# Pacing the modulation weight rows of a fused S4 + FFN kernel by product columns

## The chip, the cores and the metric

The kernel runs on one core of one Trainium2 chip. The time is device time in microseconds of one execution, the median of several; one more execution was recorded by the hardware profiler. Matrix products run on TensorE (PE), elementwise work on VectorE (DVE) and ScalarE (ACT), a few reductions over partitions on GpSimd (POOL). SyncE (SP) issues nearly all DMAs, in order: a DMA that waits for its data or its buffer holds back all that stand behind it.

## The reference, cut to what matters

x has 4 batches of 1024 channels by 2048 positions; c is 4 x 2048.

```python
mod = (_silu(c) @ wmod).reshape(4, 6, 1, -1)          # wmod: 2048 x (6*2048), 96 MB
sa, ca, ga, sb, cb, gb = (mod[:, i] for i in range(6))
# ga, gb: sign kept, magnitude at least 0.25
h = layernorm(x) * (1 + ca) + sa
x = x + ga * (causal_conv(h, K) + D[0] * h)           # K: S4 kernel of 2048 taps
h = layernorm(x) * (1 + cb) + sb
x = x + gb * (h @ W.T + bias + low_rank(h, A, Bf, coeffs * scales))
```

## The kernel before, in words

**Modulation rows.** The product with wmod is made in six sections (one for each of the six vectors) of 16 rows. A row is one load of 1 MB (`mod_load`, L309 to L313, tile `wm`, issued on SP) and four groups of products into the one PSUM tile `modps` (`mod_mm`, L317; eight matmul instructions in the profile). After the 16th row a section has a 17th step that turns `modps` into what is needed: columns `ca` (section 1), `sa` (section 0) or gates such as `gas` (section 2, `mod_gate`). The generator `section(sec, pools)` (L845) does one row for each `next`, and `take(g, n)` asks for n steps. Row buffers lie in two pools, `wmp` (three buffers) and `wms` (two); sections 1 and 0 alternate between them, sections 2 to 5 use `wmp` alone. A buffer is free when the products of its row are done.

**Convolution.** Channels are taken in 32 blocks of 128 rows. The causal convolution is a product with Toeplitz tiles of the taps, done with three products of halves in place of four, each operand split into two fp16 parts. For a block: `stats` (DVE), then `conv_prep` (normalize into `n`, transposes `tp`, scaling into `t`, the fp16 parts `hc` and `hs`), then `conv_mm` (L591): for each of two halves q, three families of matmuls (L608), into PSUM tiles `ya` and `yb`, drained by ACT (`qs`, L621, and L632 in early blocks) and DVE (L625 to L635). Five PSUM banks (`acc`) serve these, the merges (`lps`) and others. `conv_mm` calls `tick()` at nine places, where the caller slips other work into the program.

Blocks 0 to 2 are early: their gate is not there yet, so their products are kept in `y` (three buffers) and gated later by `conv_late` (L639). Blocks 0 and 1 are even run without `sa`; its share is added by `shift_conv` and `shift_add`. `conv_post` stores the gated block to `x1d` and squares into the x tile, after which block r+4 can be loaded into it.

**Kernel taps.** `toeplitz` (L233) computes the taps in steps woven into section 1 at rows `KT`. Its end is a chain through memory: `kd` is written (L253, L254), read back as overlapping rows `kb` (L258), both issued on ACT, multiplied with a reversal matrix (`kbps`) and split into `kh`, `kl`, which the first block's products need.

**Low-rank merge.** `prep_lora` (L418) loads `la` and `lb` (2 MB each) and works on them mostly on ACT. `merge` (L462), for eight column groups, makes the low-rank product (`lps`), adds it to W rows (`we`) and stores the combined weights of seven sub-products (`wcd`). The generator `rest` (L930) weaves merges and the rows of sections 4, 3 and 5; `step` (L974) advances it from block `R0` on, nine times a block by the strings of `PLAN`.

**Order.** The text order of the program is a priority. A scheduler in the framework places each instruction on its engine's list when by its own estimate its inputs are ready, the earlier in the text first. `high_priority` lifts a stretch over the rest, and `issue_after(ins)` keeps instructions on the engine of `ins` behind it. On the chip each engine then follows its list in order.

The feed-forward product (L744, blocks of `fX`, `fY`, `fZ`) follows after block 31.

Of the kernel before, what the change touches and what calls it, by code (L numbers as in the profile page):

```python
# [24 lines left out]
P = 128  # L25
# [9 lines left out]
class Net:  # L35
# [197 lines left out]
    def toeplitz(self, pool):  # L233
        nc, v = self.nc, self.nc.vector
        rev = pool.tile([P, P], F32, tag="rev", name="rev")
        nc.gpsimd.memset(rev, 0.0)
        nc.gpsimd.affine_select(
            out=rev, in_=rev, compare_op=ALU.not_equal, fill=1.0, base=1 - P, pattern=[[1, P]], channel_multiplier=1
        )
        kk = pool.tile([P, 16], F32, tag="kk", name="kk")  # L240
        yield from self.s4(pool)
        v.tensor_copy(kk, self.kp)
        dt = pool.tile([1, 1], F32, tag="dt", name="dt")
        nc.scalar.dma_start(out=dt, in_=self.io["D"].unsqueeze(0))
        v.tensor_tensor(kk[0:1, 0:1], kk[0:1, 0:1], dt, ADD)
        m = pool.tile([P, 1], F32, tag="km", name="km")
        v.tensor_reduce(m, kk, AX.X, ALU.max, apply_absolute_value=True)
        s, self.kinv = self.pow2(self.cst, self.allmax(pool, m, 1, "km"), 1, "ks")
        v.tensor_scalar(kk, kk, s, None, MUL)
        kd = self.dram.tile([P + D], F32, tag="kd", name="kd")  # L250
        z = pool.tile([1, P], F32, tag="kz", name="kz")
        v.memset(z, 0.0)
        nc.scalar.dma_start(out=kd[0:P].unsqueeze(0), in_=z)  # L253
        nc.scalar.dma_start(out=kd[P:].rearrange("(a b) -> a b", b=16), in_=kk)  # L254

        kb = pool.tile([P, D], F32, tag="kb", name="kb")
        src = bass.AP(tensor=kd.tensor, offset=kd.offset + 1, ap=[[1, P], [1, D]])
        nc.scalar.dma_start(out=kb, in_=src)  # L258
        self.kb = kb
        yield  # L260
        for q in range(4):
            ps = self.acc.tile([P, 512], F32, tag="a", name="kbps")
            nc.tensor.matmul(ps, rev, kb[:, ds(512 * q, 512)], start=True, stop=True)
            (v.tensor_copy if q % 2 else nc.scalar.copy)(kb[:, ds(512 * q, 512)], ps)


        kv = kb.rearrange("p (m e t) -> p m e t", e=2, t=P)
        ev, od = kv[:, :, 0, :], kv[:, :, 1, :]
        self.kf = {}
        for f in (0, 2, 1):  # L270
            hi = self.kpool.tile([P, HC * P], F16, tag=f"kh{f}", name=f"kh{f}")
            lo = self.kpool.tile([P, HC * P], F16, tag=f"kl{f}", name=f"kl{f}")
            h3, l3 = (x.rearrange("p (m t) -> p m t", t=P) for x in (hi, lo))
            if f == 0:
                src = ev
            else:
                src = pool.tile([P, 2, 512], F32, tag="kdif", name="kdif")
                src = src.rearrange("p a (c t) -> p (a c) t", t=P)
                if f == 1:
                    v.tensor_scalar(src[:, 0:1], ev[:, 0:1], -1.0, None, MUL)  # L280
                    v.tensor_tensor(src[:, 1:], od[:, 0 : HC - 1], ev[:, 1:], SUB)
                else:
                    v.tensor_tensor(src, od, ev, SUB)
            v.tensor_copy(h3, src)
            v.tensor_tensor(l3, src, h3, SUB)  # L285
            self.kf[f] = hi, lo
        yield
# [21 lines left out]
    def mod_load(self, pool, sec, j):  # L309
        w = pool.tile([P, D], F32, tag="wm", name="wm")  # L310
        src = self.io["wmod"].rearrange("(p j) n -> p j n", j=16)
        self.nc.sync.dma_start(out=w, in_=src[:, j, ds(sec * D, D)])
        return w  # L313

    def mod_mm(self, w, j):
# [272 lines left out]
                v.tensor_tensor(lo[:, sl], src, hi[:, sl], SUB)  # L588
            yield

    def conv_mm(self, pl, hs, x, tick, early):  # L591
        nc, v = self.nc, self.nc.vector
        hc, hs = hs
        y = pl["y"].tile([P, D], F32, tag="y", name="y")
        yv = y.rearrange("p (j e t) -> p j e t", e=2, t=P)
        if not early:
            gv = self.gat.rearrange("p (j e t) -> p j e t", e=2, t=P)
        sums = pl["sm"].tile([P, 2], F32, tag="sums", name="sums")

        def family(ps, f, q, first):  # L600
            pf = ps.rearrange("p j t -> p (j t)")
            last = 4 * q + 3
            for i in range(last + 1):
                o = P * max(0, i - 4 * q)
                k0 = P * max(0, 4 * q - i)
                for x, z in ((0, 0), (0, 1), (1, 0)):
                    h = hs[x][:, i] if f == 0 else hc[x][:, 2 * i + 2 - f]
                    nc.tensor.matmul(  # L608
                        pf[:, o:512], h, self.kf[f][z][:, ds(k0, 512 - o)],
                        start=first, stop=(i == last and (x, z) == (1, 0)), skip_group_check=True,  # L610
                    )
                    first = False
                if i == 3 and q == 1:
                    tick()

        for q in range(2):
            jj = slice(4 * q, 4 * q + 4)
            pa = self.acc.tile([P, 4, P], F32, tag="a", name="ya")
            family(pa, 0, q, True)
            qs = pl["t"].tile([P, 4, P], F32, tag="qs", name="qs")  # L620
            nc.scalar.copy(qs, pa)  # L621
            tick()
            pb = self.acc.tile([P, 4, P], F32, tag="a", name="yb")
            family(pb, 2, q, True)
            v.tensor_tensor(yv[:, jj, 1, :], pb, qs, ADD)  # L625
            if not early:
                v.tensor_tensor(yv[:, jj, 1, :], yv[:, jj, 1, :], gv[:, jj, 1, :], MUL)
            tick()
            family(pa, 1, q, False)
            sl = ds(1024 * q, 1024)  # L630
            if early:
                nc.scalar.copy(yv[:, jj, 0, :], pa)  # L632
            else:
                v.tensor_tensor(yv[:, jj, 0, :], pa, gv[:, jj, 0, :], MUL)  # L634
                v.scalar_tensor_tensor(y[:, sl], y[:, sl], 1.0, x[:, sl], MUL, ADD, accum_out=sums[:, q : q + 1])  # L635
            tick()
        return y, sums
# [167 lines left out]
ACC, TPS = 5, 2  # L805
PLAN = ("PNSL", "NL", "NSL", "NTL", "SL", "SL", "SL", "SL", "FSL", "SSL")
LPLAN = ("LL", "LL", "LL", "LL", "L", "0", "")
R0 = 3
WM, WMS = 3, 2
EARLY = 3  # L810
X0 = 11
LEFT0 = 30
KT = (0, 5, 7, 11)


def STQ(nc):
# [8 lines left out]
def net(ctx: ExitStack, tc: tile.TileContext, io):  # L825
# [19 lines left out]
    def section(sec, pools):  # L845
        for q in range(16):
            if q == 0:
                k.mod_begin()
            k.mod_mm(k.mod_load(pools[q % len(pools)], sec, q), q)
            yield  # L850
        if sec == 0:
            k.sa = k.mod_column(msm, k.kpool, "sa", 0.0)
            k.hinv = k.fold_scale(msm, k.ca, k.sa, "fs1")
        elif sec == 1:
            k.ca = k.mod_column(msm, k.kpool, "ca", 1.0)
        elif sec == 2:
            k.gas, (k.gad,) = k.mod_gate(msm, "gad")
        elif sec == 4:
            k.cb = k.mod_column(msm, k.cst, "cb", 1.0)
        elif sec == 3:  # L860
            k.sb = k.mod_column(msm, k.cst, "sb", 0.0)
        else:
            _, k.gbd = k.mod_gate(msm, "gbd", io["bias"])
        yield

    def merges():
        k.prep_lora(pl["lora"], pl["mrg"])
        yield
        for c in range(HC):
            yield from k.merge(pl["lora"], pl["mrg"], c)  # L870
# [3 lines left out]
    def take(g, n):  # L874
        for _ in range(n):
            next(g, None)
# [12 lines left out]
    def prep(r, shift=True):  # L889
        return k.conv_prep(pl, r, xs[r], sts.pop(r), hs, shift)  # L890

    def load(r):
        xs[r] = k.conv_load(pl, r)

    def stats(r):
        sts[r] = k.stats(pl, xs[r], "1")
# [8 lines left out]
        n += 1  # L905
    k.early_scale(msm)
    load(1)
    sec = section(0, (wms, wmp))
    for r in range(2):
        stats(r)  # L910
        take(prep(r, False), 9)
    take(sec, 1)
    with tc.issue_after(k.last.ins), tc.high_priority():
        take(toe, 2)
    take(sec, 1)

    def row():
        take(sec, 1)

    for r in range(2):  # L920
        ys[r] = k.conv_mm(pl, hs.pop(r), xs[r], row, True)
        load(r + 2)
    take(sec, 17)
    k.shift_conv(msm)
    k.shift_add([ys[r][0] for r in range(2)])
    st.close()
# [48 lines left out]
        if r >= R0 and "w" not in pr and next(fill, 0) == 0:  # L975
            early()

    sec = section(2, (wmp,))
    for r in range(2, EARLY + 1):
        stats(r)  # L980
    take(prep(2), 9)
    ys[2] = k.conv_mm(pl, hs.pop(2), xs[2], row, True)
    nxt = prep(3)
    take(nxt, 9)
    take(sec, 17)
    k.gat = k.gate_tile(pl["g"], 0)
    ratio = k.kpool.tile([P, 1], F32, tag="rat", name="rat")
    nc.vector.tensor_tensor(ratio, k.einv, k.hs[:, 0:1], MUL)
# [5 lines left out]
    stats(EARLY + 1)  # L994
    nxt = prep(EARLY + 1)
    take(nxt, 1)
    post = None
    for r in range(EARLY, 32):
        if EARLY + 2 < r + 2 < 32:
# [129 lines left out]
```

## Time and profile before

| | us |
|---|---|
| median of 3 runs (2148.76 to 2154.0) | 2149.32 |
| the profiled execution | 2149.26 |
| its span | 2147.5 |
| TensorE busy in the span | 2085.0 |
| VectorE busy | 1313.8 |
| ScalarE busy | 922.0 |
| data moved by DMA | 483.05 MB |

| stage before, from the trace | us from the span's start |
|---|---|
| last row of section 1 ends | 51.7 |
| block 0's first product | 66.6 |
| block 1's products end | 121.4 |
| block 2 | 136.7 to 161.0 |
| block 3 | 168.6 to 208.6 |
| last row of section 2 ends | 183.6 |
| block 4's first product | 227.5 |
| block 31's products end | 927.9 |

How to read the profile: it is one execution. A row of a group has the source line, the engine, the operation, output and inputs by name, shapes and count, then busy time and the mean of one in ns, then the idle time of the engine before these and what ended it. A row of waits reads "who <- for whom: us in total, times, longest". PEclk is the share of full clock that was granted to TensorE. Windows are in us from the span's start.

### The profile page before, as it was taken

What the parts mean: (1) busy time and instruction counts of PE and PEld (TensorE: products, weight loads), DVE (VectorE), ACT (ScalarE), POOL (GpSimd) and SP (SyncE); (2) the same over time, 40 slices, a digit from 0 to 9 for tenths busy, and PEclk for the clock granted to TensorE, in tenths of its full rate; (3) what the DMA queues carried; (4) which work ended last, traced back from release to release, by engine and by line L of the source; (5) the groups of instructions that cost most, each with busy time, mean ns of one, the idle gap of its engine ahead of it and who ended that gap; (6) DMA issues with size and microseconds to landing.
All of it is one profiled execution on the core that took longest, in us unless ns stands there. A gap on an engine that the chain in (4) does not pass through costs nothing.

```text
span 2147.5 us, 28491 instructions
## 1 busy us (share of the span) xinstructions
PE 2085.0 (97%) x11144; PEld 1028.0 (48%) x11144; DVE 1313.8 (61%) x2356; ACT 922.0 (43%) x1697; POOL 3.0 (0%) x13
## 2 busy tenths in 40 slices
PE   6998999999999999999999999999999999999999
PEld 2453445455455555554545545545444444444444
DVE  5636989988999998666566565565433323232323
ACT  1335757766677776655554454454200000000000
POOL 0000000000000000000000000000000000000000
PEclk7998999999999999999999999999999999999999
DMA  9878677767874463297465465564795545455542
GB/s 389 347 266 312 253 271 286 291 247 272 312 286 160 181 221 118 94 376 281 175 242 199 174 245 189 191 240 180 266 358 165 186 152 170 165 167 166 176 156 70
DMA packets 127142, 483.05 MB, mean 225 GB/s; under 512 B 13673, under 2 KB 13802, under 8 KB 96032
## 3 DMA queue, kind: packets, MB, share of 16 engines
q1 hardware_dynamic: 126192, 477.55, 61.1%
q10 hardware_dynamic: 816, 3.69, 0.4%
q8 instruction: 87, 1.43, 0.3%
q14 instruction: 47, 0.39, 0.0%
HBM read 325.89 MB, written 155.30 MB: 224 GB/s over the span
## 4 chain that ended last, share of the span: by engine, by line
PE 59%; DVE 6%; DMA 2%; ACT 2%; issue 1%; SPq 0%; DVEq 0%; ACTq 0%
PE fZ L744 23%; PE fY L744 15%; PE fX L744 15%; PE ya L608 3%; PE tp L694 2%; PE yb L608 1%; DVE y L635 1%; DMA xo<-x1d 1%; ACT x L654 1%; DVE wch L509 1%; DVE hc L588 1%; DVE st L535 1%; DMA w<-wcd 1%; ACT t L577 1%; DVE y L634 0%
## 5 line engine op out<-in xcount | busy, mean ns | idle before, releaser
L744 PEld LDWEIGHTS <-lf 128*128 128x128 f16 x5376 | 526.0, 98 | 620.5 <-issue 0.9
L744 PE MATMUL fZ<-w,lf 128*128 128x512 f16 x2304 | 514.1, 379 | 0.6 <-ACT p L752 0.6
L744 PE MATMUL fX<-w,lf 128*128 128x512 f16 x1536 | 342.1, 379 | 0.0
L744 PE MATMUL fY<-w,lf 128*128 128x512 f16 x1536 | 342.1, 379 | 0.0
L608 PEld LDWEIGHTS <-hc 128*128 128x128 f16 x2304 | 214.1, 98 | 208.7 <-issue 45.6
L762 DVE TENSOR_TENSOR xo<-xo,gb 128x512 f32<-128x512 f32 x128 | 87.7, 690 | 235.1 <-DMA xo<-x1d 223.6
L577 ACT ACTIVATE t<-tp,sa,ca 128x128 f32<-128x128 f32 x480 | 189.3, 474 | 20.2 <-PE tp L573 19.9
L608 PE MATMUL ya<-kh,hs 128*128 128x512 f16 (+3 forms) x768 | 195.0, 328 | 1.8 <-DVE hs L588 0.7
L608 PE MATMUL ya<-kh,hc 128*128 128x512 f16 (+3 forms) x768 | 191.7, 327 | 3.8 <-ACT qs L621 3.8
L608 PE MATMUL yb<-kh,hc 128*128 128x512 f16 (+3 forms) x768 | 190.8, 326 | 0.2
L752 ACT COPY p<-fZ 128x512 f32<-128x512 f32 x64 | 37.3, 583 | 292.6 <-PE fZ L744 275.3
L608 PEld LDWEIGHTS <-hs 128*128 128x128 f16 x1152 | 107.2, 98 | 104.2 <-issue 24.1
L696 ACT ACTIVATE gt<-tp,sb,cb 128x256 f32<-128x256 f32 x256 | 125.0, 576 | 62.5 <-PE tp L694 60.9
L752 ACT COPY p<-fX 128x512 f32<-128x512 f32 x32 | 18.8, 586 | 305.8 <-PE fX L744 227.3
L317 PE MATMUL modps<-wm,sct 128*32 128x512 f32 x768 | 119.7, 663 | 24.3 <-DMA wm<-in_wmod 16.0
L608 PE MATMUL ya<-kl,hs 128*128 128x512 f16 (+3 forms) x384 | 125.8, 328 | 0.7 <-DVE kl L285 0.7
L608 PE MATMUL ya<-kl,hc 128*128 128x512 f16 (+3 forms) x384 | 125.5, 327 | 0.0
L608 PE MATMUL yb<-kl,hc 128*128 128x512 f16 (+3 forms) x384 | 125.1, 326 | 0.0
L767 DVE TENSOR_TENSOR fin<-fX,gb 128x512 f32<-128x512 f32 x32 | 22.1, 692 | 127.3 <-PE fX L744 127.2
L481 PE MATMUL lps<-lbh,lac 128*128 128x512 f16 x256 | 87.4, 389 | 8.8 <-DVE y L634 3.3
L588 DVE TENSOR_TENSOR hc<-t,hc 128x512 f16<-128x512 f32 x128 | 87.7, 685 | 8.7 <-ACT hc L587 8.6
L573 PE MATMUL tp<-ident,n 128*128 128x128 f32 x512 | 79.2, 280 | 13.8 <-ACT t L577 9.8
(259 smaller groups left out, 2230.8 us busy)
## 6 DMA issues: line engine op xcount, KB each, us to landing
wm<-in_wmod SPq DMA_DIRECT2D x96, 1024.0 KB
lfd<-lf SPq DMA_DIRECT2D x112, 512.0 KB
lf<-lfd SPq DMA_DIRECT2D x112, 512.0 KB
x<-in_x SPq DMA_DIRECT2D x32, 1024.0 KB
x1d<-y SPq DMA_DIRECT2D x32, 1024.0 KB
x<-x1d SPq DMA_DIRECT2D x32, 1024.0 KB
xo<-x1d SPq DMA_DIRECT2D x128, 256.0 KB
out<-xo SPq DMA_DIRECT2D x128, 256.0 KB
```

The source lines that it names most:

```text
L317: self.last = self.nc.tensor.matmul(self.modps[32 * g : 32 * g + 32, :], self.sct[:, j].rearrange("p r b -> p (r b)"), w[:, ds(512 * g, 512)],
L481: nc.tensor.matmul(ps, la[:, x, k, h], y[:, k, osl], start=(n == 0), stop=(n == 5))
L573: nc.tensor.transpose(tp[:, k], n[:, ds(P * (c0 + k), P)], self.ident)
L577: nc.scalar.activation(t[:, k], tp[:, k], AF.Identity, bias=self.sa[:, c, b : b + 1], scale=self.ca[:, c, b : b + 1],)
L588: v.tensor_tensor(lo[:, sl], src, hi[:, sl], SUB)
L608: nc.tensor.matmul(pf[:, o:512], h, self.kf[f][z][:, ds(k0, 512 - o)], start=first, stop=(i == last and (x, z) == (1, 0)), skip_group_chec ...
L694: nc.tensor.transpose(tp[:, c, r], xs[r][:, ds(P * (c0 + c), P)], self.ident)
L696: nc.scalar.activation(t[:, c0 + c], tp[:, c], AF.Identity, bias=self.sb[:, c0 + c, b : b + 1], scale=self.cb[:, c0 + c, b : b + 1],)
L744: nc.tensor.matmul(ps[name], lf[i][:, k, x, :], wc[i][k // 4][:, k % 4, y, :], start=(first and n == 0), stop=(n == 3 * HC - 1), skip_grou ...
L752: nc.scalar.copy(t, ps[name])
L762: v.tensor_tensor(x, x, self.gbias[:, h], ADD)
L767: v.tensor_tensor(t, cv, self.gbt[:, h], MUL)
```

## The change

- The three DMAs of `kd` and `kb` are issued on POOL instead of ACT, and the third and fourth step of the tap computation stand one row earlier (`KT`).
- Sections 0 and 2 become one stream `rows`. It is no longer advanced at the ticks of the early blocks, but by `pace`, called after each set of matmuls of `conv_mm` with the number of columns multiplied: every `ROWC` = 3700 columns give one step. It runs through blocks 0, 1 and 2.
- Loads of blocks 0 to 3 are kept on SP behind the latest row load that the text has reached (`lastw`), and blocks 2 and 3 are asked for ahead of the products of blocks 0 and 1 instead of behind them.
- Statistics and preparation of block 2 stand ahead of the shift sums; those of block 3 go into the ticks of block 2.
- `prep_lora` is asked for once, by `next(fill)` ahead of the loop over blocks 3 to 31, and its SP loads stand behind the last row of section 2.
- The merges, and with them the rows of sections 4, 3 and 5, begin at block 5 instead of block 3 (`R0`).

```diff
@@ toeplitz
-        nc.scalar.dma_start(out=kd[0:P].unsqueeze(0), in_=z)
-        nc.scalar.dma_start(out=kd[P:].rearrange("(a b) -> a b", b=16), in_=kk)
+        nc.gpsimd.dma_start(out=kd[0:P].unsqueeze(0), in_=z)
+        nc.gpsimd.dma_start(out=kd[P:].rearrange("(a b) -> a b", b=16), in_=kk)
...
-        nc.scalar.dma_start(out=kb, in_=src)
+        nc.gpsimd.dma_start(out=kb, in_=src)
@@ mod_load
-        self.nc.sync.dma_start(out=w, in_=src[:, j, ds(sec * D, D)])
+        self.lastw = self.nc.sync.dma_start(out=w, in_=src[:, j, ds(sec * D, D)])
@@ conv_mm
-    def conv_mm(self, pl, hs, x, tick, early):
+    def conv_mm(self, pl, hs, x, tick, early, pace=lambda n: None):
...
                 if i == 3 and q == 1:
                     tick()
+                pace(3 * (512 - o))
@@ constants
-R0 = 3
+R0 = 5
+ROWC = 3700
-KT = (0, 5, 7, 11)
+KT = (0, 5, 6, 10)
@@ net: merges, load
-        k.prep_lora(pl["lora"], pl["mrg"])
+        with tc.issue_after(k.lastw.ins):
+            k.prep_lora(pl["lora"], pl["mrg"])
...
-        xs[r] = k.conv_load(pl, r)
+        if r < 4:
+            with tc.issue_after(k.lastw.ins):
+                xs[r] = k.conv_load(pl, r)
+        else:
+            xs[r] = k.conv_load(pl, r)
@@ net: blocks 0 and 1
-    sec = section(0, (wms, wmp))
+    rows = (x for sec, w in ((0, (wms, wmp)), (2, (wmp,))) for x in section(sec, w))
...
-    take(sec, 1)
+    take(rows, 1)
     with tc.issue_after(k.last.ins), tc.high_priority():
         take(toe, 2)
-    take(sec, 1)
-
-    def row():
-        take(sec, 1)
+    take(rows, 1)
+    cols = [0]
+
+    def pace(n):
+
+        cols[0] += n
+        while cols[0] >= ROWC:
+            cols[0] -= ROWC
+            take(rows, 1)
 
     for r in range(2):
-        ys[r] = k.conv_mm(pl, hs.pop(r), xs[r], row, True)
         load(r + 2)
-    take(sec, 17)
+        ys[r] = k.conv_mm(pl, hs.pop(r), xs[r], lambda: None, True, pace)
+    stats(2)
+    take(prep(2), 9)
     k.shift_conv(msm)
     k.shift_add([ys[r][0] for r in range(2)])
@@ net: block 2, ahead of the loop
-    sec = section(2, (wmp,))
-    for r in range(2, EARLY + 1):
-        stats(r)
-    take(prep(2), 9)
-    ys[2] = k.conv_mm(pl, hs.pop(2), xs[2], row, True)
+    stats(3)
     nxt = prep(3)
+    ys[2] = k.conv_mm(pl, hs.pop(2), xs[2], lambda: take(nxt, 1), True, pace)
     take(nxt, 9)
-    take(sec, 17)
+    take(rows, 40)
...
     take(nxt, 1)
+    next(fill)
     post = None
```

## The prediction

> **What bounds the kernel now.** I read the page's busy shares and slices first, then finer stretches of the first 400 us, then whom TensorE waited for in the stretch that stood out, then single rows of the timeline.
>
> ```profile
> PE 2085.0 (97%) x11144; PEld 1028.0 (48%) x11144; DVE 1313.8 (61%) x2356; ACT 922.0 (43%) x1697; POOL 3.0 (0%) x13
> PE   6998999999999999999999999999999999999999
> PEclk7998999999999999999999999999999999999999
> ```
>
> TensorE is busy 2085.0 of 2147.5 us. The change removes no product, so all that it can win is idle time (62.5 us in all) and time at a lowered clock. Both lie in the first slices. The next answer gives stretches of those: width, TensorE busy, granted clock, DMA share, GB/s.
>
> ```profile
> 16.00:56.00 40.00, 29.47 (x152) 0.67 0.99 403
> 66.00:136.00 70.00, 69.28 (x446) 0.98 0.78 295
> 136.00:158.00 22.00, 21.60 (x136) 1.00 0.72 279
> 158.00:186.00 28.00, 20.15 (x138) 0.89 0.99 368
> 186.00:197.00 11.00, 11.00 (x42) 0.83 0.70 270
> 197.00:213.00 16.00, 13.50 (x79) 1.00 0.70 251
> 213.00:224.00 11.00, 7.62 (x21) 0.53 0.99 371
> 224.00:262.00 38.00, 37.16 (x223) 1.00 0.59 227
> 278.00:284.00 6.00, 5.63 (x16) 0.72 0.65 257
> 284.00:400.00 116.00, 116.00 (x722) 1.00 0.73 269
> ```
>
> The reader is to see three regimes. To 56 us the DMA is full (0.99) and weight rows set the pace. From 66 to 158 TensorE is full while the DMA is only 0.72 to 0.78 busy: transfer time is thrown away. From 158 to 186 that is paid back: DMA full, TensorE waiting. Who it waits for from 136 to 290:
>
> ```profile
> PE modps L317 <- DMA wm<-in_wmod: 8.3, 7, 4.6
> PE lps L481 <- DVE y L634: 3.3, 1, 3.3
> PE lps L481 <- DVE y L625: 2.5, 1, 2.5
> PE tp L573 <- ACT t L577: 2.3, 2, 2.0
> PE lps L481 <- ACT lbh L456: 2.1, 1, 2.1
> PE lps L481 <- DVE we L483: 0.5, 1, 0.5
> ```
>
> With 0.3 us on hs these are 19.3 us of idle. Half clock adds: 1.4 in 158:186 (the last three rows took 1.56, 1.94 and 1.94 instead of 1.06), 11 x 0.17 = 1.9 in 186:197, 7.62 x 0.47 = 3.6 in 213:224, 6 x 0.28 = 1.7 in 278:284: 8.6 us. So 136 to 290 loses 27.9 us. 284:400 is full; the small waits later (some 16 us up to 960) I hold for unchanged by a shift of two blocks.
>
> **The change part by part.**
>
> *Paced rows.* A row of section 0 or 2 is one 1 MB load and 8 matmuls, 1.06 us together in the timeline. At 403 GB/s a load takes 1.049 MB / 403 = 2.60 us. A block's products have 3 x 3 x (1280 + 3328) = 41,472 columns (the two halves of L603 to L612), and 24 matmuls of 512 take 5.18 us in the chain, so a block is 17.5 us and 3,700 columns are 1.56 us. One row per 3,700 columns is thus a row per 1.56 + 1.06 = 2.62 us, just what the DMA delivers. Three blocks give 33.6 pulls; 32 are needed after the two taken ahead. The last row's matmuls fall at 92% of block 2. Before, 5 of the 16 gate rows were still to come when block 3 began (168.6 us). Now none is. Removed: the row waits from 158 to 183 (0.24 + 0.33 + 0.42 + 0.15 + 1.64 + 0.94 = 3.7) and the half clock they led to (1.4 + 1.9): 7.0 us.
> Added: section 2 still has three buffers (section 0 five), so a row's load is issued when the matmuls three rows earlier end, 7.8 - 1.06 = 6.7 us before it is needed. In the trace, with three in flight, loads issued at 172.05 and 174.63 were waited for at 179.16 and 181.66, some 7.0 us. It is a near thing, but 8 us of work without rows (shift sums, transposes) lets the ring refill. I take 2 us; the ends are 0, and 13 rows x 0.5 = 6.5.
> SP's queue: x2 and x3 (1 MB each) now stand ahead of rows instead of behind, one slot of 2.6 us each; five landed rows cover that.
>
> *Low-rank loads behind the gate's rows.* la (2 MB) was issued at 116.1 and lb at 147.9, amid the rows. Taken out, they free 10 us of DMA, and ACT, which held prep(3) up by 2.03 us and the first merge by 2.10: 4.1 us removed. What is late next is prep_lora itself, after the last row. Its ACT work, from 120 to 200:
>
> ```profile
> L447 ACT ACTIVATE lsq<-lb 128x1024 f32<-128x1024 f32 x4 | 4.3, 1078 | 0.1
> L432 ACT ACTIVATE la<-la 128x2048 f32<-128x2048 f32 x2 | 3.9, 1962 | 0.0
> L455 ACT ACTIVATE lb<-lb,lsb_s 128x2048 f32<-128x2048 f32 x2 | 3.9, 1994 | 1.2 <-DVE lsb_s L55 1.2
> L443 ACT ACTIVATE lb<-lb,lwt 128x2048 f32<-128x2048 f32 x2 | 3.9, 1993 | 0.0
> L456 ACT CAST lbh<-lb 128x2048 f16<-128x2048 f32 x2 | 3.7, 1886 | 0.0
> ```
>
> That is 19.7 us (21 with its small rows), now beside the posts' Squares (3 x 2.0) and the preparation of blocks 4 and 5.
>
> *Merges from block 5.* Blocks 3 and 4 lose the filler: the lps waits on y and we (6.4 us) and the half clock of 213:224 (3.6) go: 10.0 us removed. The merge work itself is only moved, from blocks 3 to 23 to blocks 5 to 25, with left units from block 30 on: nothing for that. But the chain from the last row to block 4 is now bare. Before, it took from 183.6 (last row) to 195.5 (gate tile), 208.3 (x4 load issued, once y0 is gated and x0 squared), 222.0 (n) and 227.5 (first product of block 4): 43.9 us. Without the lbh casts and lbl ahead of the gate (about 6), the two merge evictions (1.5) and a row or so of TensorE (1.5), I put it at 35. With row waits the last row is at about 170, block 4 at 205. TensorE has from 172 (end of block 2) 17.5 us of block 3, 3.9 of gps and 2 of transposes: it is done at 195.5. Added: 9.5 us idle. Bounds: 4 if gate and posts run without a queue; 9.5 + 8 if prep_lora's ACT work stands ahead of the posts and t.
> After such a gap the array is cold. The trace's row is 213:224: after 2.5 and 3.3 us of idle it cost 3.6 us. The Trainium skill, "TensorE: Matmul & The Clock Gate", section "The HAM clock gate", says that about 3.4 us of sustained work restores full clock, which by estimate is 1.7 us lost. It also speaks against this change: one long gap surely trips the gate, several short ones may not. I take the row's 3.6, and 1 for VectorE's backlog, which this row shows (197 to 228: DVE 30.51 of 31):
>
> ```profile
> 197.00:228.00 31.00, 24.33 (x117) 10.31 (x114) 30.51 (x67) 10.71 (x21) 0.00 (x0) 0.83 0.85 317
> ```
>
> The 4.6 us wait at 273.8 with its 1.7 came when a row's load stood on SP behind wcd stores that waited for VectorE. With less backlog half of it may go: 3 us removed (0 to 6.3).
>
> *Kernel taps on POOL, one row earlier.* The second s4rp set is moved from behind row 7 to behind row 6, and the last stage from 11 to 10; s4rp started at 30.57, so kd can be issued some 1.8 us sooner than 43.4. ACT no longer holds for kd (its r_t sat until 50.8, and x0's statistics 6.1 us with it); cae at 57.6 comes some 2 us sooner. On POOL, km_r and es_r are the neighbours: es_r started at 55.05, and kb is issued once kd has landed (7.0 us before, 43.4 to 50.4), well ahead of it. Against it speaks the Trainium skill, "SBUF — State Buffer", section "SBUF: two separate sides": a POOL DMA has its descriptors written by GpSimd, and VectorE ops in two-port mode lock it out; 0.62 us became 3.1. No POOL DMA is in this trace; its POOL rows take 0.4 us. By the rule two dependent transfers lose up to 5 us and block 0 starts 3 us late; by the trace, in which queueing (7 and 10 us) is nearly all of the time, it starts 1.5 us early. I take 0.5 gained: -1.5 to +3.
>
> **Sum.** Removed 7.0 + 4.1 + 10.0 + 3.0 + 0.5 = 24.6. Added 2 + 9.5 + 3.6 + 1 = 16.1. Net -8.5. The profiled execution took 2149.26 us (span 2147.5 and 1.8 around it), the median is 2149.32, so no correction: 2140.8, say 2141.
>
> **Rivals.**
> A, as summed, 0.55: 2141, own range 2133 to 2148.
> B, the gap stays small, 0.13: idle 4, no cold array, no SP stall: 2149.3 - 21.6 - 6.3 + 2 + 4 = 2127. For it: ACT is busy only 10.71 us in 197:228.
> C, the change does not do what it says, 0.12: rows are not on time because three buffers can't hold 2.62 us (13 x 0.5 = 6.5), and the kernel taps come 3 us late: 8.5 - 4.5 - 3.5 = 0.5 left, 2149. For it: the 7.0 us of landing against 6.7. Against: the DMA's 0.72 in 136:158.
> D, slower, 0.20: ACT's order. prep_lora stands ahead of the loop in the program, so its 21 us are issued among the posts and the preparations of blocks 4 and 5, whose t and casts are 10 us a block. ACT then sets the pace of two blocks without filler: 8 us more before block 4, 6 before block 5, and 2.5 cold: 2141 + 16.5 = 2157.5. It decides from where block 4's first product comes later than 213.5 (205 + 8.5). For it: the wait on t at 165 behind the lb pass. Against: ACT had 20 us to spare in 197:228.
>
> **How the numbers follow.** The prediction is A's. 0.3% is 6.4 us, about what a measurement of this kernel can tell from no change: faster is below 2142.9, slower above 2155.8. Faster: 0.40 of A, 0.13 of B, 0.02 of C = 0.55. Slower: 0.02 of A, 0.02 of C, 0.18 of D = 0.22. Same: 0.23. The range runs from B's 2127 to D's 2157.
>
> **What would show it.** Right: no wait of modps on wm beyond 0.5 us from 66 to 170, DMA near 0.95 there, la issued after the last gate row, the last gate row at 168 to 172, one TensorE gap of 6 to 12 us ahead of block 4, the two lps waits gone. D: waits of tp on t or of ya on hc behind lb rows. C: modps waits of 0.3 to 1 us at every gate row, or a first ya later than 68. I am wrong if the gap before block 4 is over 15 us or if a new wait of over 5 us shows after 300 us.

## The result and the profile after

| | before | after |
|---|---|---|
| median of 20 runs each, us | 2151.73 | 2148.75 |
| span of the profiled execution, us | 2147.5 | 2145.5 |
| TensorE busy in it, us | 2085.0 | 2077.9 |
| TensorE idle in it, us | 62.5 | 67.6 |

The ratio of after to before is 0.9987, interval 0.9980 to 0.9993: 2.8 us faster (1.5 to 4.3), a third of the 8.5 us forecast. TensorE idles 5.1 us *more* and is busy 7.1 us less.

The page of the kernel after: busy shares, then TensorE and its granted clock in 40 slices.

```profile
PE 2077.9 (97%) x11144; PEld 1027.8 (48%) x11144; DVE 1309.7 (61%) x2356; ACT 927.8 (43%) x1697; POOL 5.1 (0%) x16
...
PE   6997899999999999999999999999999999999998
...
PEclk8998899999999999999999999999999999999999
```

The fourth digit (161 to 215 us) fell from 8 to 7 and the fifth (215 to 268 us) from 9 to 8: the hole in TensorE's work moved, it did not close. The kernel after in the stretches shown of before (width, TensorE busy, granted clock, DMA share, GB/s):

```profile
16.00:56.00 40.00, 27.68 (x152) 0.74 0.99 406
66.00:136.00 70.00, 66.90 (x442) 0.99 0.82 309
136.00:158.00 22.00, 22.00 (x145) 0.88 0.64 226
158.00:186.00 28.00, 27.24 (x161) 1.00 0.87 300
186.00:197.00 11.00, 7.63 (x55) 0.95 0.96 360
197.00:213.00 16.00, 5.39 (x24) 0.71 0.96 388
213.00:224.00 11.00, 3.90 (x16) 0.50 0.87 341
224.00:262.00 38.00, 36.68 (x223) 0.92 0.45 170
278.00:284.00 6.00, 6.00 (x42) 1.00 0.49 178
284.00:400.00 116.00, 114.41 (x712) 1.00 0.73 272
```

158:186 is full (27.24 of 28, before 20.15) and 278:284 too. But 197:224, which had 21.12 us of TensorE work before, has 9.29. Whom TensorE waits for from 136 to 290 us in the kernel after:

```profile
PE tp L573 <- DVE lsb_i L54: 11.0, 1, 11.0
PE tp L573 <- ACT t L577: 7.3, 2, 6.5
PE ya L608 <- ACT qs L622: 3.4, 1, 3.4
PE gps L669 <- DVE mg L347: 0.8, 1, 0.8
PE modps L317 <- DMA wm<-in_wmod: 0.8, 1, 0.8
```

The row waits (8.3 us before) are down to 0.8 and all waits of lps (8.4) are gone. In their place stand 17.5 us ahead of block 4's transposes, and 3.4 us of block 3's last products on ScalarE's copy `qs`. There is no wait at all from 228 to 290 us. The four stretches of work ahead of block 4, with the idle time before each and what ended it:

```profile
213.38 1.97 PE L573 MATMUL tp<-ident,n 128*128 128x128 f32 x8 [10.99 <-DVE lsb_i L54]
216.10 1.93 PE L317 MATMUL modps<-wm,sct 128*32 128x512 f32 x8 [0.75 <-DMA wm<-in_wmod]
224.52 1.11 PE L573 MATMUL tp<-ident,n 128*128 128x128 f32 x4 [6.49 <-ACT t L577]
226.44 1.11 PE L573 MATMUL tp<-ident,n 128*128 128x128 f32 x4 [0.80 <-ACT t L577]
```

The first of these names `lsb_i`, a short VectorE row that merely came last; what block 4's transposes need is `n`, made from x4 until 213.33 us.

*A measure for the rest.* I gave each matmul instruction the median spacing of its form in the kernel before, and a row's eight matmuls together the 1.00 us from its first to the next instruction, so that every kernel has the same 2038.5 us of TensorE work. "Loss" is time passed minus work done: idle, half clock, and wider spacing. The column "change forecast" is the forecast's sum, put to its stages.

| stage, us | loss before | loss after | change forecast | change measured |
|---|---|---|---|---|
| to 136 | 40.4 | 40.1 | -0.5 | -0.3 |
| 136 to 186 | 12.0 | 5.0 | -7.2 | -6.9 |
| 186 to 228 | 13.9 | 27.2 | +2.2 | +13.3 |
| 228 to 290 | 9.4 | 1.1 | -3.0 | -8.3 |
| 290 to 930 | 27.0 | 27.1 | 0 | +0.1 |
| from 930 | 0.9 | 1.0 | 0 | +0.1 |
| sum, with rounding | | | -8.5 | -2.1 |

At 290 us the changed kernel is 2.2 us ahead and it stays there. One stage went 11.1 us worse than forecast, another 5.3 us better.

### The profile page after: what moved, and what is told of

Read it like the earlier page. It is cut to its first block, busy times and chain, and to the rows that moved or that the text cites. A ratio compares the mean times of both kernels' runs of the same rounds, so it can differ in the third digit from the quotient of the medians.

```text
span 2145.5 us, 28479 instructions
## 1 busy us (share of the span) xinstructions
PE 2077.9 (97%) x11144; PEld 1027.8 (48%) x11144; DVE 1309.7 (61%) x2356; ACT 927.8 (43%) x1697; POOL 5.1 (0%) x16
## 3 DMA queue, kind: packets, MB, share of 16 engines
q0 software_dynamic: 208, 1.06, 0.1%
## 4 chain that ended last, share of the span: by engine, by line
PE 65%; DVE 13%; ACT 8%; issue 2%; DMA 2%; DVEq 0%; ACTq 0%
PE fZ L745 23%; PE fX L745 15%; PE fY L745 15%; PE ya L608 5%; PE tp L695 3%; PE yb L608 2%; ACT t L577 2%; DVE wch L509 2%; ACT x L655 2%; DVE st L535 2%; DVE y L636 1%; DVE hc L588 1%; ACT we L500 1%; PE lps L481 1%; DVE n L552 1%
## 5 line engine op out<-in xcount | busy, mean ns | idle before, releaser
L697 ACT ACTIVATE gt<-tp,sb,cb 128x256 f32<-128x256 f32 x256 | 125.0, 576 | 62.5 <-PE tp L695 60.9
L753 ACT COPY p<-fX 128x512 f32<-128x512 f32 x32 | 18.8, 586 | 305.8 <-PE fX L745 241.7
L317 PE MATMUL modps<-wm,sct 128*32 128x512 f32 x768 | 115.2, 660 | 19.9 <-DMA wm<-in_wmod 12.6
L588 DVE TENSOR_TENSOR hc<-t,hc 128x512 f16<-128x512 f32 x128 | 87.5, 683 | 12.0 <-ACT hc L587 11.8
```

The source lines that it names most:

```text
L317: self.last = self.nc.tensor.matmul(self.modps[32 * g : 32 * g + 32, :], self.sct[:, j].rearrange("p r b -> p (r b)"), w[:, ds(512 * g, 512)],
L697: nc.scalar.activation(t[:, c0 + c], tp[:, c], AF.Identity, bias=self.sb[:, c0 + c, b : b + 1], scale=self.cb[:, c0 + c, b : b + 1],)
L753: nc.scalar.copy(t, ps[name])
```

## The experiments

Ratios are to the kernel before on the same chip, with their 95% intervals. The milestones that decide between the readings, in us from the start of each span:

| | gate's last row done | x4 load issued | x4's statistics | first transpose of block 4 | first product of block 4 | gate row to product |
|---|---|---|---|---|---|---|
| before | 183.7 | 208.3 | 214.1 | 223.5 | 227.5 | 43.9 |
| after | 174.1 | 193.2 | 205.0 | 213.4 | 227.3 | 53.2 |
| e2_r0_5 | 185.3 | 206.1 | 213.5 | 222.3 | 226.2 | 40.9 |
| e4_fill_later | 175.5 | 194.5 | 206.1 | 214.0 | 218.8 | 43.3 |
| e5_lora_early | 183.2 | 208.9 | 216.7 | 224.8 | 228.7 | 45.5 |
| e6_lora_behind_x5 | 176.3 | 193.0 | 198.8 | 209.3 | 213.5 | 37.2 |

**The parts alone: e1_taps, e2_r0_5, e3_rows.** The kernel before with one part of the change. In e3 the taps, the place of `prep_lora` and R0 are as before, and only the paced rows and the order of loads and preparations remain. The fourth part, `prep_lora` behind the gate's rows, was not run alone.

```diff
 e1:  kd, kb issued by gpsimd; KT = (0, 5, 6, 10)
 e2: -R0 = 3
     +R0 = 5
 e3 (against after): taps, prep_lora and R0 as before
```

> The kernel before with the kernel-tap part of the change alone: kd and kb issued on POOL, third and fourth tap step one row earlier. In the changed kernel block 0's first low-part product came at 68.2 us instead of 68.65. Theory (the taps were never far from the rest of block 0's inputs): 0 to 1 us faster, first ya within 1 us of 66.6. Rival (POOL's DMAs dear): first ya 2 to 3 us later, 2 to 3 us slower.

Measured: 1.0009 (0.9999 to 1.0018), no gain, and no sign of dear DMAs on POOL. The transfers themselves did what was hoped. POOL in the kernel after, 30 to 66 us (start, length, line, operation, idle before and its releaser):

```profile
41.00 0.74 POOL L254 DMA_DIRECT2D kd<-kk  x1 [1.34 <-DVE kk L249]
46.73 0.55 POOL L258 DMA_DIRECT2D kb<-kd  x1 [4.99 <-DMA kd<-kk]
```

kd is issued at 41.00, before at 43.4, and kb 5.7 us later, before 7.0. By the last update of its semaphore kb had landed at 56.75, before at 60.54. But in e1 block 0's first product came at 67.4 (66.6 before), with a row wait of 3.6 us at 53.75. The same wait stands in after (4.1 us at 52.16); in e10_no_taps below it is not, and smaller waits on `mrow` and `t` (2.0 and 1.6 us) are in its place. On TensorE's list the products of kb (L263) stand behind that row: in after they begin at 60.26, before at 60.69, so nearly all of what kb gained is lost there. So the wait goes with this part; why the row is late was not tried.

> The kernel before with merges begun at block 5 (R0 = 5) and nothing else. Theory (merges in blocks 3 and 4 fed the backlog of VectorE and the row stuck on SP behind wcd stores): the lps waits on y (6 us), the half clock after them and the 4.6 us wait at 273.8 go, and some of it comes back as a gap before block 4 of 5 to 8 us; net 6 to 8 us faster at 300 us, less at the end if two more merged blocks at the end cost what the changed kernel lost from 300 to 930 us (5 us): 1 to 3 us faster. Rival (filler is worth more than backlog): gap before block 4 of over 15 us, no change or slower.

Measured: 0.9973 (0.9964 to 0.9982). One constant gains twice what the whole change does. Its waits from 136 to 290 us:

```profile
PE tp L573 <- DVE n L552: 14.9, 1, 14.9
PE modps L317 <- DMA wm<-in_wmod: 5.2, 5, 3.2
PE tp L573 <- ACT t L577: 2.8, 2, 2.1
```

The two lps waits and the wait at 273 us are gone here too. So they went with the later merges, without any pacing. And e2 has the gap ahead of block 4 as well: 14.9 us, where 5 to 8 were expected. The total is 6 us faster than before, twice the upper end of what was expected.

> The changed kernel with taps, prep_lora and R0 put back as before: only the rows of sections 0 and 2 are paced by columns, and the early loads and preparations reordered. Theory (rows are the sound part): no wait of a row on its load from 66 us on beyond 2 us in sum, last gate row at 174 to 177, 7 us less lost at 186 us than before, about 5 to 7 us faster at the end. Rival (la and lb, again among the rows, cost what pacing wins): row waits of 4 us or more after 140, 0 to 2 us faster.

Measured: 1.0013 (1.0004 to 1.0021), slower, against both texts. No row waits on its load from 60 to 186 us and the gate's row comes at 177.1, as the theory had it. But with the merges still at block 3, the wait for n is 17.9 us at 195.70 and block 4 starts at 241.7. The three parts alone sum to -0.05%, which with these intervals agrees with the whole change's -0.13%.

**What stands in the gap: e4_fill_later, e5_lora_early, e6_lora_behind_x5.** Three places for `prep_lora`.

```diff
 e4: -    next(fill)                 # ahead of the loop
     +        if r == 4:             # at the top of block 4 in the loop
     +            next(fill)
 e5:  next(fill) ahead of stats(3) and block 2, without issue_after
 e6:  as e4, and
     -        with tc.issue_after(k.lastw.ins):
     +        with tc.issue_after(k.x5.ins):   # the load of x5
                  k.prep_lora(...)
```

> The changed kernel with prep_lora asked for at the top of block 4 instead of ahead of block 3, so that on ACT the t and casts of block 4 stand ahead of most of its passes over lb. Theory (ACT order: in the changed kernel t waited from 214 to 223 us behind L443 to L456): the wait of tp on t (6.5 and 0.8 us) goes, block 4's first product at 217 to 220 instead of 227.3, 6 to 8 us faster than the changed kernel. Rival (x4's late landing sets the gap: issued at 193.2, statistics only at 205): block 4's first product not before 224, within 3 us of the changed kernel.

Measured: 1.0007 (0.9999 to 1.0015). Block 4 starts where the theory had it, but the total is worse, not better. ScalarE in the kernel after, 200 to 232 us:

```profile
201.92 1.99 ACT L443 ACTIVATE lb<-lb,lwt 128x2048 f32<-128x2048 f32 x1
...
205.80 1.04 ACT L447 ACTIVATE lsq<-lb 128x1024 f32<-128x1024 f32 x1
...
215.61 3.88 ACT L455 ACTIVATE lb<-lb,lsb_s 128x2048 f32<-128x2048 f32 x2
219.39 3.68 ACT L456 CAST lbh<-lb 128x2048 f16<-128x2048 f32 x2
222.98 1.83 ACT L577 ACTIVATE t<-tp,sa,ca 128x128 f32<-128x128 f32 x5
```

and in e4:

```profile
214.21 2.00 ACT L443 ACTIVATE lb<-lb,lwt 128x2048 f32<-128x2048 f32 x1
216.12 1.84 ACT L577 ACTIVATE t<-tp,sa,ca 128x128 f32<-128x128 f32 x5
...
221.88 1.12 ACT L447 ACTIVATE lsq<-lb 128x1024 f32<-128x1024 f32 x1
...
228.04 2.02 ACT L443 ACTIVATE lb<-lb,lwt 128x2048 f32<-128x2048 f32 x1
```

In after the first `t` of block 4, whose transposes are there from 213.38 on, stands behind 7.4 us of L455 and L456. In e4 it stands ahead of all but one of the passes over lb, and block 4 starts 8.5 us earlier. But it then lasts from 218.8 to 253.9, with a row wait of 3.1 us at 239.6. The loss by 228 us is 5.7 less than in after (66.6 against 72.3), by 250 us 1.4 more (74.8 against 73.4): all of it comes back within one block.

> The changed kernel with prep_lora asked for ahead of block 2 and not held behind the gate's rows, so that la and lb come in amid block 2, where the changed kernel's DMA was 0.64 busy and ACT idle. Theory (the gap before block 4 is set by what the late low-rank loads do to x4's landing and to t): from the gate's last row to block 4's first product 41 to 45 us, as in the kernel with R0 = 5 alone (40.9), instead of 53.2; last gate row at 174 to 179; block 4 at 217 to 222; 5 to 9 us faster than the changed kernel, about 2141 to 2145. Rival (the rows lose what the loads gain): gate's last row after 180, block 4 after 223, no faster than the changed kernel.

Measured: 1.0013 (1.0005 to 1.0021), as the rival had it. With la issued at 133.2 and lb at 156.1 amid the rows, the gate's last row came at 183.2, 9 us later than in after. And VectorE copied the finished rows only at 190.4, behind its own low-rank work, which had waited for ScalarE:

```profile
182.14 1.06 PE L317 MATMUL modps<-wm,sct 128*32 128x512 f32 x8
...
185.05 4.49 DVE L457 TENSOR_TENSOR lbl<-lb,lbh 128x2048 f16<-128x2048 f32 x2 [3.38 <-ACT lbh L456]
...
190.40 0.68 DVE L342 COPY mg<-modps 128x512 f32<-128x512 f32 x1
```

> As the run with prep_lora asked for at block 4, but la (and so lb) is loaded only behind x5's load on SP. Theory (DMA: lb and the section rows in flight made x4 take 12 us to land): x4's statistics 6 to 8 us after its issue instead of 11.6, block 4's first product at 212 to 215 instead of 218.8. Rival (other transfers, stores of y and rows, fill the DMA as well): block 4 at 217 or later. At the end the low-rank work is later still, so the first merge waits for lbh and the total may be 0 to 5 us slower.

Measured: 1.0057 (1.0044 to 1.0070), the slowest. Its start is the best of all, as the theory had it, by the landing of x4. SyncE's queue in after, 186 to 216 us:

```profile
188.03 5.06 SPq L651 DMA_DIRECT2D x1d<-y  x2
193.18 3.28 SPq L557 DMA_DIRECT2D x<-in_x  x2
```

and in e6:

```profile
192.96 0.35 SPq L557 DMA_DIRECT2D x<-in_x  x1
194.37 0.33 SPq L653 DMA_DIRECT2D x1d<-y  x1
```

x4 is issued at the same time in both. By the last of the 16 updates of its semaphore in the trace it had landed at 203.8 in after and at 198.7 in e6: 10.6 and 5.8 us behind its issue (10.3 in e4, which differs from e6 only in when la and lb are loaded). The statistics begin at 205.0 and 198.8; in after VectorE had other work until then, so the last 1.2 us are not the landing's. In after lb (2.1 MB, issued at 185.4) and two stores (1 MB each) are ahead of x4. They landed at 199.1, 198.9 and 201.4. With x4 they are 5.2 MB, by estimate 13 us at the 403 GB/s of the first stage; the load ahead of them had landed at 191.0, which gives 204. In e6 neither lb nor the second store is ahead of x4. But there `la` starts at 205.8, rows wait 11.6 us in all, and block 4 lasts to 270.0.

**The start of the merges: e7_r0_4, e8_r0_7, s4_r0_6, e12_after_r0_3.** The kernel before with R0 = 4, 7 and 6, and the changed kernel with R0 = 3.

```diff
-R0 = 3        # before          -R0 = 5        # after, e12
+R0 = 4, 7, 6  # e7, e8, s4      +R0 = 3
```

> The kernel before with merges from block 4. Theory (what the first merge meets is VectorE's backlog from conv_late, at its height in block 3): lps waits on y gone, some of the gain of R0 = 5: 3 to 5 us faster than before. Rival (the gain of R0 = 5 came from the 4.6 us row wait alone): that wait stays in the 260s to 280s and the run is within 1.5 us of before.

> The kernel before with merges from block 7. Theory (backlog is worked off by block 5): no further gain up to 320 us over R0 = 5, and more lost from 300 to 930 us; 2146 to 2150. Rival (the later the better): 2143 or less.

> The kernel before with R0 = 6 alone. R0 gave 0 at 3, -0.12% at 4, -0.27% at 5, -0.17% at 7. Theory (what R0 saves are the waits of the first merges ahead of 290 us, and each later start pushes merges and their small waits into later blocks): -0.2 to -0.27%. Rival (5 was a lucky placement of one order): -0.12 to -0.17%, the same as at 4 and 7.

> The changed kernel with merges begun at block 3 again, all else as changed. Theory (the later merges are what the change gains by): the first merges wait for the late low-rank work, 5 to 10 us slower than the changed kernel, 2153 to 2159, slower than before. Rival (the merges' place matters little once rows are paced): within 2 us of the changed kernel.

Measured: R0 = 4 0.9988 (0.9978 to 0.9998), 6 0.9987 (0.9978 to 0.9996), 7 0.9983 (0.9976 to 0.9990), against 0.9973 for 5. So any later start gains some 0.12 to 0.17%, and 5 a further 0.1% that its neighbours do not show; the rival of the run with 6 was right, and why 5 is better stays open. In e7 the lps waits are gone, as its theory had it, and so is the wait at 273 us; e8's median, 2146.6, lies in its theory's range. In the changed kernel R0 = 3 gives 1.0028 (1.0018 to 1.0038), as its theory had it: without the later merges the rest of the change costs 0.28%. The wait for n is 20.2 us there.

**Sizes of the change: e9_rowc_3200, e10_no_taps, e11_no_taps_3200, s3_five_buffers.** The changed kernel with a row per 3200 columns; with the taps as before; with both; and with section 2's rows on five buffers.

```diff
 e9, e11:  -ROWC = 3700
           +ROWC = 3200
 e10, e11:  kd, kb issued by scalar; KT = (0, 5, 7, 11)
 s3:       -(2, (wmp,))
           +(2, (wms, wmp))     # the low-rank pools open behind block 2
```

> The changed kernel with a row every 3200 columns instead of 3700, so that the last gate row falls at 80% of block 2 instead of 92%. Theory (after pacing, the chain from the gate's last row to block 4 sets the end, so an earlier gate is worth its time): gate's last row at 168 to 171 instead of 174, block 4's first product 3 to 6 us sooner than 227.3, 2 to 5 us faster than the changed kernel. Rival (rows come no faster than the DMA, 2.6 us a row): row waits of over 3 us between 66 and 170, gate no sooner than 173, the same or slower.

> The changed kernel with the kernel-tap part put back (kd and kb on ACT, KT as before). Theory (parts add up: taps alone cost 0.09%): 1 to 3 us faster than the changed kernel, 2146 to 2148, no 4.1 us wait for a row at 52 us. Rival (the taps part is only paid where rows are not paced): within 1 us of the changed kernel or slower.

> Both: taps put back and a row every 3200 columns. Theory: the two gains add up, 2142 to 2146, at or below the kernel with R0 = 5 alone (2145.7). Rival (each only moves the wait): 2147 or more.

> The changed kernel with section 2's rows on five buffers (both pools) in place of three; the low-rank pools open behind block 2 for that. What sets the 3.2 us between the rows of section 2? Theory three buffers: a load may not be issued until the products three rows back are done, so five let rows come every 2.6 us, the gate's last row at 168 or earlier, and loads are issued earlier by up to two rows. Theory static order (the scheduler's own estimate put the rows 3.2 us apart on TensorE's list): loads are issued earlier, the last row still comes at 173 to 175. In both block 4 stays near 227 and the time within 0.15% of the changed kernel, since x4's landing and ACT's order set it, unless the gate's row sets x4, then block 4 comes as much earlier as the row.

Measured: 0.9988 (0.9979 to 0.9997), 0.9991 (0.9983 to 0.9999), 0.9991 (0.9983 to 0.9998) and 0.9994 (0.9985 to 1.0003): none differs from the 0.9987 of the changed kernel by more than its interval, so the rivals of the first three were right. The gate's last row came at 177.1, 174.7, 174.0 and 177.1 (block 0 itself started 1.7 us later in s3). TensorE's rows in after:

```profile
163.34 1.06 PE L317 MATMUL modps<-wm,sct 128*32 128x512 f32 x8
...
166.61 1.06 PE L317 MATMUL modps<-wm,sct 128*32 128x512 f32 x8
...
169.77 1.07 PE L317 MATMUL modps<-wm,sct 128*32 128x512 f32 x8
...
172.99 1.06 PE L317 MATMUL modps<-wm,sct 128*32 128x512 f32 x8
```

and in s3:

```profile
166.35 1.06 PE L317 MATMUL modps<-wm,sct 128*32 128x512 f32 x8
169.62 1.06 PE L317 MATMUL modps<-wm,sct 128*32 128x512 f32 x8
172.77 1.06 PE L317 MATMUL modps<-wm,sct 128*32 128x512 f32 x8
175.99 1.06 PE L317 MATMUL modps<-wm,sct 128*32 128x512 f32 x8
```

They come 3.2 us apart in both, with no wait ahead of one and products between them. With 3200 columns (e9, e11) the spacings of these rows are the same to 0.01 us. In s3 the loads were issued 11.7 to 14.8 us ahead of their use, in after 8.5. So neither 3700 columns, nor three buffers, nor the DMA (0.64 to 0.87 busy) sets this. It is the order written on TensorE's list, as the second theory of s3 had it. By what reckoning the scheduler came to it was not tried.

**Side by side: s1_after_again, s2_r0_5_again.** The changed kernel and R0 = 5 alone on one chip.

```diff
 s1: none                       s2: -R0 = 3
                                    +R0 = 5
```

> The changed kernel itself, unedited, on the same chip as the next run, so that the whole change and its R0 part alone can be set against each other. Theory (the gain is R0's, the paced rows cost): some 3 us behind the kernel before with R0 = 5 alone, ratio to before 0.9985 to 0.9993 against 0.9970 to 0.9978. Rival (the difference seen between the two calls was that of chips and rounds): the two within 1 us of each other.

> The kernel before with R0 = 5 alone, on the same chip as the changed kernel. Theory: ratio to before 0.9970 to 0.9978, 3 us ahead of the changed kernel, as the whole loss of the changed kernel up to 228 us is no less (121.9 against 121.7 us) though its gate's row comes 11 us earlier. Rival: no difference, both near 0.998.

Measured: 0.9990 (0.9981 to 1.0000) and 0.9967 (0.9954 to 0.9979), medians 2151.91 and 2144.74. R0 = 5 alone beats both kernels, by 7 us where 3 were expected. By 228 us s1 has lost 73.2 and s2 70.7 us, although s1's gate comes 8 us earlier. From 290 to 930 us s1 loses 30.3 and s2 24.6. So most of the difference between the two lies in the later blocks, where no experiment looked for it; the cause is open.

## Why the forecast was wrong

*Row waits and half clock (7.0): the size was right, the cause only in part.* The loss from the start to 186 us fell by 7.3 (52.4 to 45.1), where the forecast's terms for these stages make 7.7. (Of the three slow rows that it names the trace has two, 1.56 and 1.94 us, which make its 1.4.) But R0 = 5 alone has 6.0 of this (46.4), and the rest of the change with R0 = 3 (e12) only 1.6. So the first merges had been in the rows' way as much as the order of the rows. That the size came out is in part luck. Of the forecast's signs, DMA near 0.95 from 66 to 170 failed: it was 0.82, 0.64 and 0.87.

*"The last row's matmuls fall at 92% of block 2": wrong, twice.* By the text the gate's last row is the 31st pull, at some 80% of block 2. And the step took the text's order, 3700 columns and 1.06 us, for the order on the engine. Rows came every 3.2 us instead of 2.62, the last one 1.4 us behind block 2's end (171.6), 4 us later than the 170 in the sum. The ring of three, which was blamed beforehand, was innocent (s3).

*The gap before block 4 (9.5 + 3.6 + 1 = 14.1): the step that failed.* Block 4 was forecast at 205 and came at 227.3. The stage from 186 to 228 us lost 13.3 us more than before, not 2.2. The idle time of the gap was 19.0 us, not 9.5, and the 3.4 us on `qs` were in no step. The chain of 35 us from gate row to block 4 was made from that of before by taking work away. By the table of milestones the chain measured, in us:

| | gate row to x4's load | load to statistics | statistics to transposes | transposes to product | sum |
|---|---|---|---|---|---|
| before | 24.6 | 5.8 | 9.4 | 4.0 | 43.8 |
| after | 19.1 | 11.8 | 8.4 | 13.9 | 53.2 |
| e4_fill_later | 19.0 | 11.6 | 7.9 | 4.8 | 43.3 |
| e6_lora_behind_x5 | 16.7 | 5.8 | 10.5 | 4.2 | 37.2 |

The work taken away gave 6.5 of the 9 us hoped for; two links grew by 16. Shown to have been left out: that ScalarE runs prep_lora's passes ahead of block 4's `t` (e4, which moves them, starts block 4 8.5 us earlier), and that lb, moved out of the rows, now lands on top of x4 (5 us, e6 against after or e4). With both away (e6) the chain is 37.2, near the 35 of the forecast. The first is rival D's mechanism, and block 4 came 13.8 us later than the 213.5 from which D was to decide. The second was nowhere in the text: the DMA was priced where the loads left, not where they arrived. ScalarE and VectorE changed places in 197 to 228 us; the kernel after:

```profile
197.00:228.00 31.00, 11.97 (x50) 6.04 (x49) 24.95 (x70) 25.48 (x37) 0.36 (x1) 0.61 0.87 342
```

ScalarE 25.48 of 31 where it had 10.71, VectorE 24.95 where it had 30.51.

*Yet D's total (2157.5) was wrong too.* D kept the gains of R0 at the forecast's size. The loss from 228 to 290 us fell by 8.3 us, not 3.0: the wait at 273.8 went whole, and with it the half clock behind it. Both went with R0 alone (e2: 2.0 left there). That this error helped where the gap hurt is luck; it is why the total missed by less than 6 us and not by 11.

*"Later waits unchanged": right.* From 290 to 930 us TensorE idles 14.05 us (before 15.38), longest wait 1.5, and the loss is 27.1 (before 27.0). The changed kernel has 352 of the row matmuls in this stretch where before had 310: that is work moved behind 290 us, not loss. Two traces of the changed kernel (after, s1) differ here by 3.2 us, so smaller changes can't be read from one.

*Cold clock (3.6): right size.* By the timeline of after, 1.97 + 1.93 + 1.11 us of work ran at half clock between the gaps (eight transposes take 1.09 us at full clock, at 162.37 in before), then 226.44 to about 230.05 without a break: 8.6 us, 4.3 lost. The last stretch, 3.6 us, agrees with the rule of the Trainium skill, "TensorE: Matmul & The Clock Gate", section "The HAM clock gate", which the forecast drew on (about 3.4 us of sustained work). What it missed is that three gaps in a row keep the clock down through all of the short work between them.

*Taps (0.5): within its bounds, no gain.* e1 is 1.9 us slower (interval -0.2 to +3.9), and POOL's DMAs took 0.74 and 0.55 us. The loss that the forecast feared by the skill's rule did not show, but the rule was not put to the test: VectorE was at its statistics (L535) at 41.00 and idle at 46.73.

Put together: an earlier gate can't help while x4, ScalarE's list and the merges stand behind it. After reaches the gate 11 us before e2 and starts block 4 1.2 us behind it. From the issue of x4 it takes 34.1 us where e2 takes 20.1: 4.4 more to the statistics, 10.0 more between transpose and product.

## What to carry to other kernels

When a load is moved out of a crowded stretch, follow it to where it lands and list what else lands there; here the price was paid at that place. When two engines' lists are written by a scheduler, a count of columns in the text need not say when the work runs (here 3700 and 3200 gave the same spacing): read the spacing from a trace of the kind of order that will be used. And try the one-constant part of a change alone before crediting the elaborate part.

## What the hardware showed that was not expected

The clock was lowered while TensorE counted as busy all the time. In after the shift sums' 32 thin matmuls (16 columns down to 1) run inside block 2:

```profile
132.13 4.66 PE L397 MATMUL gsp<-sae,kb 128*128 128x16 f32 x32
136.65 0.59 PE L608 MATMUL yb<-kl,hc 128*128 128x512 f16 x1
137.03 0.63 PE L608 MATMUL yb<-kh,hc 128*128 128x512 f16 x1
...
139.73 1.84 PE L317 MATMUL modps<-wm,sct 128*32 128x512 f32 x8
...
143.85 1.06 PE L317 MATMUL modps<-wm,sct 128*32 128x512 f32 x8
```

and the granted clock in the three microseconds behind them (busy 3.00 of 3.00, clock 0.50, DMA 0.01):

```profile
137.00:140.00 3.00, 3.00 (x16) 0.50 0.01 3
```

A row takes 1.84 us there and the next one 1.06. Before, the same 32 matmuls stood between blocks (121.27, 3.68 us), TensorE was busy without a break from 121 to 128 us, and the clock was 1.00 to 125 and 0.50 behind it. That the clock falls behind these matmuls as it does behind idle time was in no step of the forecast. What in them does it (few columns, fp32, the weight loads) was not tried. The DMA stands nearly still in the same stretch (0.01, 3 GB/s), in a kernel whose gate waits for rows: the loads issued at 125.2, 128.8 and 132.0 fill the three buffers, and their products come at 139.7, 143.9 and 147.3.
